# Reload order in the last image, and the place of p's nested weights in image 0: attention and a non-local block on one core

## The chip, the cores and the metric

The kernel runs on one core of one Trainium2 chip. The metric is the device time of one execution in microseconds (us), median of three runs; everything is float32. Five engines work side by side: TensorE (PE: matrix products, with its weight loads as PEld), VectorE (DVE), ScalarE (ACT), GpSimd (POOL) and SyncE (SP), which here starts nearly all transfers. Each engine takes its instructions in the order in which the built program has them.

## The reference

Eight images of 512 channels and 32 x 32 = 1024 positions pass two layers. Cut to what matters:

```python
# layer 0: attention, 8 heads of 64
q, k, v = (conv1x1(x, W, b).reshape(B, 8, 64, N) for W, b in ((Wq, bq), (Wk, bk), (Wv, bv)))
attn = softmax(einsum('bhdn,bhdm->bhnm', q, k) * 64 ** -0.5)
x = x + conv1x1(einsum('bhnm,bhdm->bhdn', attn, v).reshape(B, C, H, W), Wp, bp)
# layer 1: a non-local block, 256 inner channels, then batch normalization over all images
g, theta, phi = (conv1x1(x, W, b) for W, b in ((g_w, g_b), (theta_w, theta_b), (phi_w, phi_b)))
f = einsum('bcn,bdn->bcd', theta, phi) / N
z = conv1x1(einsum('bcd,bdn->bcn', f, g), W_w, W_b) + x
out = (z - mean(z)) * rsqrt(var(z) + 1e-5) * gamma + beta     # over images and positions
```

The mean and the variance of z need all eight images. So z of each image has to be kept until the last image is done, and only then can outputs be written.

## The kernel before, in words

**Stages.** One loop runs over the images. In each turn come attention (`attention`), then q, v and k of the next image (`heads_of`, `values`), the projection p with its residual (`project`), theta and phi together (`theta_phi`, tile `tp`), and the non-local block (`nonlocal_`: g, then f, then z). Products of 512 channels are computed with seven block products in place of eight (`seven`), in the order

```python
SEVEN = (("11", 0, "11", 0, (("11", True),)), ("s1t1", 3, "t1", 1, (("22", True),)),
         ("s2t2", 4, "t2", 0, (("12", True),)), ("s4", 6, "22", 1, (("12", False),)), ...
```

The second entry is the block of the weight, the third the block of the data, the fourth the PSUM slot. The first product uses weight block 0, the second block 3, the third block 4, the fourth block 6. The third adds to the slot of the first, so it waits until VectorE has read that slot. The argument `between` is a dictionary: after the product of that number, and after its PSUM was read, its function puts further instructions into the program.

**Weights.** Blocks 3 to 6 are sums and differences of the four quarters (`weight_sums`, L107). Some products are cut once more, by the same scheme, into blocks of 128 columns; their weights are "nested" (`nest`, L211: four operations of 128 x 128 for each block). In image 0 both kinds are computed, and the finished ones are written to DRAM (`keep`, L206, tensors `kept_...`); from then on they are only loaded (`fetch` L168, called by `load_w`). A weight comes in up to three units: for theta/phi these are blocks 1 and 2 (with nested weights), blocks 3, 4 and 5, and block 6. A unit goes into one of four buffers of pool `wr` and can be loaded only when the unit that was there before has been read for the last time. `load_w` takes the next unit of a list written ahead.

**Queue.** SP starts the transfers in program order. A start that has to wait, for a buffer or for an earlier transfer, holds up all starts behind it. Eight semaphores count landings of these transfers in turn, so each start also waits until the one eight places ahead has landed.

**z.** z of images 0 to 5 is written to DRAM (`spill`), with g and the product W f of images 5 and 6 (`spill_g`). In the last turn they are read back as buffers become free:

```python
def reload(b, pool, tag):            # four transfers of 512 KB (L961)
    t = pool.tile([P, CC, N], F32, tag=tag, name=f"z_{b}")
    for cc in range(CC):
        sp(nc.sync.dma_start(t[:, cc, :], spill[b][:, cc, :]))
```

Images 0, 1, 2 and 3 go to the places of v, q, k and `fold`; image 5 comes in four chunks (`reload_chunks`, L968), then g and W f of images 5 and 6 (`take_back`, L955), image 4 at the end. `last_z` (`late_unit`, L978) computes z of images 5 to 7 chunk by chunk, and `finish` (L1019, L1017, L1020) normalizes all eight and writes them.

**Lines.** Product matmuls stand at L365 (the helper `seven`), nested ones at L313. VectorE's reads of theta/phi's products are L795 (first) and L800 (added), those of p L760 and L471.

## Time and profile before

| | us |
|---|---|
| three runs | 2117.17, 2117.42, 2118.31 |
| median | 2117.42 |
| profiled execution: its time | 2116.34 |
| profiled execution: its span | 2114.6 |
| TensorE busy | 2085.1 |
| VectorE busy | 1428.3 |
| ScalarE busy | 789.9 |
| GpSimd busy | 584.9 |

The span is the time from the first to the last instruction of the profiled execution; its own time holds 1.7 us more around it. Rows of the profile give source line, engine, operation and tiles as out<-in, the count, busy time, mean duration of one, and the idle time before with what ended it. A releaser is the instruction or transfer that ended a wait. The granted clock of TensorE is given as a share of full speed; over the span it is 0.994. A float32 matmul of the source appears as two in the trace.

### The profile page before, as it was taken

The page shows a single profiled execution, that of the slowest core. Times are in us where ns is not written, and L with a number is a line of the kernel's source. Part 1 is how long each engine was busy: PE and PEld are TensorE (multiplying, and loading weights), DVE is VectorE, ACT ScalarE, POOL GpSimd, SP SyncE. Part 2 cuts the span into 40 slices and gives each one's busy share as a digit, 9 for nine tenths or more (in the row PEclk, how much of TensorE's full clock was granted, in tenths as well). Part 3 has the DMA queues.
Part 4 walks back from the last instruction along what each step waited for, and adds up shares of the span by engine and source line. Part 5 has one row for each costly group of instructions (what it writes and reads, how often), then busy time and mean ns, then how long its engine had stood idle before and what let it go on. Part 6 is the DMA issues. An engine that isn't in the chain of part 4 may idle for free.

```text
span 2114.6 us, 33849 instructions
## 1 busy us (share of the span) xinstructions
PE 2085.1 (99%) x13654; PEld 1173.4 (55%) x13654; DVE 1428.3 (68%) x2144; ACT 789.9 (37%) x1045; POOL 584.9 (28%) x454
## 2 busy tenths in 40 slices
PE   9999999999999999999999999999999999999996
PEld 4535864357733677337763377633875348733462
DVE  6587567775678656786567766777665775567736
ACT  1464204642046410564106631166303652066016
POOL 0012900128101371015611156011650129211000
PEclk9999999999999999999999999999999999999998
DMA  6253534244232532425324253232534235222848
GB/s 229 83 148 80 175 115 145 41 93 143 105 116 40 116 115 104 120 41 140 117 73 125 41 153 109 98 95 39 170 129 157 41 73 167 74 32 40 281 181 320
DMA packets 72883, 246.74 MB, mean 117 GB/s; under 512 B 12816, under 2 KB 21264, under 8 KB 70672
## 3 DMA queue, kind: packets, MB, share of 16 engines
q1 hardware_dynamic: 61792, 218.16, 30.6%
q0 software_dynamic: 9072, 24.78, 9.5%
q8 instruction: 110, 1.80, 0.3%
q10 hardware_dynamic: 1856, 1.56, 0.3%
q14 instruction: 53, 0.43, 0.1%
HBM read 163.20 MB, written 47.71 MB: 100 GB/s over the span
## 4 chain that ended last, share of the span: by engine, by line
PE 95%; DMA 2%; DVE 1%; ACT 1%; issue 0%; SPq 0%; DVEq 0%
PE po L627 21%; PE ps L601 21%; PE ptp L365 7%; PE pv_in L441 6%; PE pq_in L444 6%; PE pk_in L444 6%; PE pp L365 6%; PE pg L365 4%; PE pz L365 3%; PE ptp_in_s L313 2%; PE pf L844 2%; PE pp_in_s L316 2%; PE pq L411 1%; PE pv L365 1%; PE pv L408 1%; PE pq L365 1%
## 5 line engine op out<-in xcount | busy, mean ns | idle before, releaser
L604 ACT ACTIVATE e<-ps 128x1024 f32<-128x1024 f32 x512 | 522.6, 1024 | 422.5 <-PE ps L601 411.8
L610 DVE TENSOR_TENSOR acc<-acc,e 128x1024 f32<-128x1024 f32 x384 | 470.0, 1224 | 103.5 <-ACT e L604 94.0
L601 PE MATMUL ps<-q,k 64*64 64x512 f32 x4096 | 529.3, 589 | 0.0
L627 PE MATMUL po<-e,v 64*64 64x512 f32 x4096 | 528.6, 589 | 0.0
L640 POOL DMA_DIRECT2D fold<-acc x189 | 144.7, 766 | 1183.4 <-DMA fold<-acc 753.2
L627 PEld LDWEIGHTS po<-e,v 64*64 64x64 f32 x4096 | 156.6, 133 | 282.9 <-issue 275.7
L601 PEld LDWEIGHTS ps<-q,k 64*64 64x64 f32 x4096 | 155.5, 133 | 283.5 <-issue 275.6
L887 ACT ACTIVATE g<-pg,gb 128x512 f32<-128x512 f32 x31 | 21.3, 687 | 445.8 <-PE pg L365 445.7
L608 DVE TENSOR_TENSOR acc<-e,e 128x1024 f32<-128x1024 f32 x64 | 78.3, 1224 | 118.4 <-ACT e L604 116.2
L365 PE MATMUL ptp<-w_tp,t_x 128*128 128x256 f32 x400 | 98.2, 386 | 6.3 <-DMA w_tp<-kept_tp 6.3
L365 PE MATMUL pp<-t_o,w_WpT 128*128 128x512 f32 x208 | 101.0, 592 | 0.0
L365 PEld LDWEIGHTS ptp<-w_tp,t_x 128*128 128x128 f32 x400 | 73.7, 194 | 15.0 <-issue 6.7
L452 DVE TENSOR_TENSOR v<-v,pv_in 128x256 f32<-128x256 f32 x112 | 46.2, 421 | 43.8 <-PE pv_in L441 37.3
L452 DVE TENSOR_TENSOR k<-k,pk_in 128x256 f32<-128x256 f32 x112 | 46.8, 421 | 39.4 <-PE pk_in L444 34.9
L365 PE MATMUL ptp<-w_tp,x 128*128 128x256 f32 x272 | 69.6, 380 | 0.0
L365 PE MATMUL pp<-o,w_WpT 128*128 128x512 f32 x144 | 67.7, 592 | 0.0
L450 ACT COPY v<-pv_in 128x256 f32<-128x256 f32 x84 | 31.4, 374 | 95.8 <-DVE T_pv L452 25.5
L450 ACT COPY k<-pk_in 128x256 f32<-128x256 f32 x84 | 31.3, 372 | 91.6 <-PE pk_in L444 90.0
L707 POOL TENSOR_TENSOR o<-o,r 128x1024 f32<-128x1024 f32 x28 | 65.2, 2367 | 0.0
L760 DVE SCALAR_TENSOR_TENSOR x<-pp,bp,x 128x512 f32<-128x512 f32 x52 | 37.6, 746 | 33.3 <-PE pp L365 33.3
L441 PE MATMUL pv_in<-w_WvT,i_t_x 128*128 128x128 f32 x448 | 59.2, 275 | 0.0
L444 PE MATMUL pk_in<-i_t_x,w_WkT 128*128 128x256 f32 x224 | 57.8, 381 | 0.0
(246 smaller groups left out, 3118.9 us busy)
## 6 DMA issues: line engine op xcount, KB each, us to landing
fold<-acc POOLq DMA_DIRECT2D x189, 128.0 KB, 3.0
w_WqT<-kept_WqT SPq DMA_DIRECT2D x21, 896.0 KB, 5.7
w_WvT<-kept_WvT SPq DMA_DIRECT2D x21, 896.0 KB, 4.9
w_WkT<-kept_WkT SPq DMA_DIRECT2D x21, 896.0 KB, 5.9
r<-den_d SPq DMA_DIRECT2D x32, 512.0 KB, 6.7
x<-in_x_dram SPq DMA_DIRECT2D x30, 512.0 KB, 6.1
spill<-x SPq DMA_DIRECT2D x24, 512.0 KB, 4.1
z<-spill SPq DMA_DIRECT2D x24, 512.0 KB, 10.4
```

Of the source, the lines that this page charges most:

```text
L365: pe(nc.tensor.matmul(to_ps, lhsT(k), rhs(k), start=(s, at) not in begun, stop=(k == nk - 1), skip_group_check=True))
L441: pe(nc.tensor.matmul(ps[:, i, :], d[:, i * P:(i + 1) * P], a, start=start and not i, stop=True, skip_group_check=True))
L444: pe(nc.tensor.matmul(ps, a, d, start=start, stop=True, skip_group_check=True))
L450: nc.scalar.copy(piece(q, i, j), ps)
L452: dve(nc.vector.tensor_tensor(piece(q, i, j), piece(q, i, j), ps, ALU.add))
L601: pe(nc.tensor.matmul(ps[c * P // 2:(c + 1) * P // 2, j, :], k[r, p, keys], q[r, p, h * 512:(h + 1) * 512], start=True, stop=True, skip_gr ...
L604: nc.scalar.activation(e, ps, AF.Exp, scale=SCALE)
L608: nc.vector.tensor_tensor(accs[u], es[u, 0], e, ALU.add)
L610: ins = nc.vector.tensor_tensor(accs[u], accs[u], e, ALU.add)
L627: pe(nc.tensor.matmul(ps[j * D:(j + 1) * D, r, :], v[keys, m, (2 * p + j) * D:(2 * p + j + 1) * D], e[keys, j, :], start=(m == 0), stop=(m ...
L640: nc.gpsimd.dma_start(to, part_of, accum_op=ALU.add)
L707: dve((engine or nc.vector).tensor_tensor(at, at, of, ALU.mult))
```

## The change

It has two parts, one at each end of the loop.

In the last turn, the reloads of z of images 2 and 3 (eight starts on SP) move from ahead of the projection to behind the loads of the remaining units: theta/phi's second and third unit and g's one unit.

In image 0, the nested weights of p (both blocks) are made after theta/phi's second product, instead of after the third and the fourth; and block 6 of theta/phi's weights is made after the third product instead of after the second. In the built program VectorE then has: read of the second product, eight nest operations, read of the third product, block 6, read of the fourth. Before, it had: read of the second, block 6, read of the third, four nest operations, read of the fourth, four nest operations. On SP the write of p's nested unit comes ahead of that of theta/phi's block 6. No instruction is added or removed.

```diff
             put_away(b - 1)
-            for i, tag in enumerate("vqk"):
+            for i, tag in enumerate("vq"):
                 reload(i, mats, tag)
-            reload(3, foldp, "fold")
         if not last:
             tpb = load_tpb(b)
         w = weights("WpT", sums_done=True)
...
         load_w("first")
         load_w(times=3 if b else 2)
+        if last:
+            reload(2, mats, "k")
+            reload(3, foldp, "fold")
...
         if b == 0:
             weight_sums(w, corner["tp"], (3, 4, 5), dve)

-            between.update({1: lambda: weight_sums(w, corner["tp"], (6,), dve), 2: lambda: nest(w_p, 1),
-                            3: lambda: nest(w_p, 2)})
+            between.update({1: lambda: (nest(w_p, 1), nest(w_p, 2)), 2: lambda: weight_sums(w, corner["tp"], (6,), dve)})
         tp = theta_phi(b, w, data, tpb, between)
```

## The prediction

> **What bounds the kernel now.** I read the page's busy shares first, then the waits of TensorE, then the stages that the change touches as timelines, then the same stage of three images as windows. In the page's part 1 and in the waits (releaser, total us, times, longest):

> ```profile
> PE 2085.1 (99%) x13654; PEld 1173.4 (55%) x13654; DVE 1428.3 (68%) x2144; ACT 789.9 (37%) x1045; POOL 584.9 (28%) x454
> ```

> ```profile
> PE count L1204 <- DVE good L1202: 8.6, 1, 8.6
> PE ptp L365 <- DMA w_tp<-kept_tp: 6.3, 1, 6.3
> ...
> PE pg L365 <- DVE w_WgT L107: 0.7, 1, 0.7
> ```

> TensorE runs back to back for the whole span. A stall put into it or taken out of it moves the end by its own length, as long as the last outputs follow it. The 8.6 us wait is the final check, after the last product. The only large stall is 6.3 us of theta/phi in the last image, on weights still in transfer. Its place on TensorE and on SP's queue (start, length, op, count):

> ```profile
> 2001.34 3.62 PE L365 MATMUL ptp<-w_tp,x 128*128 128x256 f32 x16
> 2011.23 9.20 PE L365 MATMUL ptp<-w_tp,t_x 128*128 128x256 f32 x32 [6.28 <-DMA w_tp<-kept_tp]
> ```

> ```profile
> 1985.41 13.91 SPq L961 DMA_DIRECT2D z<-spill  x12
> 2000.32 1.60 SPq L168 DMA_DIRECT2D w_tp<-kept_tp  x2
> 2002.88 0.32 SPq L168 DMA_DIRECT2D w_WgT<-kept_WgT  x1
> ```

> SP starts sixteen z transfers of 512 KB before it comes to the weights. The chain of waits says why they take so long: each start waits until the transfer eight places ahead has landed.

> ```profile
> 1981.26 7.91 DMA z<-spill
> ...
> 1989.19 11.07 DMA z<-spill
> ...
> 2000.32 10.78 DMA w_tp<-kept_tp
> ```

> The theta/phi stage from its first product to g's first, as windows (length, busy TensorE, granted clock, DMA share, GB/s): images 5 and 6, then 7; and the stall's surroundings.

> ```profile
> 1569.54:1593.12 23.58, 23.58 (x138) 1.00 0.47 176
> 1815.16:1838.75 23.59, 23.59 (x137) 1.00 0.24 80
> 2001.34:2033.48 32.14, 25.86 (x137) 0.89 0.64 249
> ```

> ```profile
> 2008.57:2011.23 2.66, 0.00 (x0) 0.03 (x1) 0.00 (x0) 0.00 (x0) 2.58 (x5) 0.50 1.03 414
> 2011.23:2015.40 4.17, 4.17 (x10) 3.37 (x11) 0.00 (x0) 0.00 (x0) 1.11 (x2) 0.50 1.02 409
> ```

> The stage takes 8.55 us more in image 7. The wait is 6.28; another 4.17 x 0.5 = 2.09 went because the clock had fallen to half and came back only at 2015.40. The rest, 0.2, is the slow first matmuls.

> [...]

> **Part A, the last image.** Eight of the sixteen z starts (images 2 and 3) now follow three weight starts: theta/phi's second unit (768 KB), its third (256 KB) and g's (896 KB). In the built program the second unit's start waits for the first z's landing (1981.26 + 7.91 = 1989.17) and for p's fifth product, whose buffer it takes. p's seven products start at 1977.30 and take 3.43 us each, so that one ends at 1994.5. The third unit waits for the sixth product (1997.9), g's weights for the seventh (2001.34).

> When does the second unit land? Before, the ninth z landed at 2000.26 with eight ahead of it; at 1.28 us for 512 KB (409 GB/s) the eight were in by 1999.0. 768 KB more is 1.9 us: about 2001, the third unit 0.6 later. The second is needed when the first product ends, 2001.34 + 3.45 = 2004.8; the third at 2011.7. The latest I can make it is the longest landing of a z transfer in this stage, 11.7 us: 1994.5 + 11.7 = 2006.2, a stall of 1.4 and too short for the clock. I take no stall.

> What is late next? The third product adds to a bank that VectorE reads from 2006.31 to 2007.53; TensorE reaches it at 2008.24, 0.7 later. GpSimd's inner sums start at 2006.62 and the first four end at 2009.5, before 2011.7. So the stage should take image 6's 23.59: **-8.55 us** for A.

> Behind the wait of g's weights stand eight z, four chunks of image 5's z, WwT and the reloaded g and W f of images 5 and 6. From 2001.34 they are 2.2 us for g's weights and 13 x 1.28 = 16.6: drained near 2020, landed by 2022. The first reloaded g waits for the fourth theta/phi product (start at 2027.04 before, 2018.5 now), the second for a later one. With 12 us to land they are in by about 2036. TensorE reads them at 2052.41 - 8.55 = 2043.9, so the cover is 8 us. z of images 2 and 3 is read first by ScalarE near 2066.1 - 8.55. Without that cover each microsecond late would be a microsecond. The output stage is bound by transfers (399 GB/s from 2070), but between 2040 and 2050 nothing moves and its first output waits for the last image's statistics, so it comes forward too.

> **Part B, image 0.** Nothing is added: four operations of 128 columns for each of two nested blocks, and one sum of 512 columns (w_tp, block 6), change places on VectorE. The order before (timeline of VectorE):

> ```profile
> 286.42 1.23 DVE L795 TENSOR_TENSOR tp<-ptp,tpb 128x1024 f32<-128x1024 f32 x1
> 287.56 0.68 DVE L107 TENSOR_TENSOR w_tp<-w_tp,w_tp 128x512 f32<-128x512 f32 x1
> 289.87 1.23 DVE L795 TENSOR_TENSOR tp<-ptp,tpb 128x1024 f32<-128x1024 f32 x1 [1.63 <-PE ptp L365]
> 291.01 1.26 DVE L211 TENSOR_TENSOR w_WpT<-w_WpT 128x128 f32<-128x128 f32 x4
> ```

> The sum was ready at 288.24; theta/phi's fourth product, which reads it, began at 289.67. In the built order of the changed kernel the read of the second product is followed by all eight nest operations, then the read of the third product, then the sum; the fourth product waits for the sum. So: nests from 287.56, 2 x 1.26 less an overlap of 0.08, to 290.0; the read of the third product (its matmuls are done at 289.87) occupies 1.14 until the next start, 291.15; the sum 0.68, to 291.85; TensorE starts 0.15 later, as after the w_WgT sum (ends 305.91, matmul at 306.06): 292.0. TensorE stalls 292.0 - 289.67 = 2.3 us, and with a slow first matmul **+2.35 us**.

> No later slack takes it up. VectorE's next reads are released by TensorE (idle 1.05, 1.05, 2.2 before them), so they move with it, and the 0.7 us wait for w_WgT hangs on a VectorE chain that starts with such a read. SP writes the nested block back at about 290 instead of 295.75, and the loads behind it start about 4 us earlier; worth nothing, since the only wait of the g stage is on VectorE. Bounds for B: zero is excluded by the order; above, the clock. Gaps of 0.7 us leave it at 1.00 and one of 6.28 halves it; 2.35 is between and unmeasured. One window at half clock would cost 1.7, two 3.4. [...] I take no clock loss.

> **Sum.** -8.55 + 2.35 = -6.2 us. The profiled execution: span 2114.6 to 2108.4, its time 2116.34 to 2110.1. The median of the runs shown is 1.1 above that execution, so 2117.42 - 6.2 = **2111.2 us**.

> **Rivals.**
> 1. The clock halves in image 0 as well. [...] 2111.2 + 1.7 to 3.4 = 2112.9 to 2114.6.
> 2. A new wait takes A's place: the weights land after 2004.8, or the output stage does not come forward. For: weights took 10.8 us to land before, and outputs move at 399 GB/s. Against: half the queue ahead of them is gone, and the stage's start is released by TensorE. If A gives 2 to 6 us, 2113.8 to 2117.8.
> 3. Slower: the reloads behind g's weights come too late for image 5's z at 2043.9. Place: the first pz of image 5. It decides from the moment the second reloaded g lands 8 us after my 2036; it eats the gain at 14 us and is slower than the measurement can miss at 18. For: thirteen transfers are behind one wait now. Against: they need 19 us and have 42. With 20 us late, 2117.42 + 5.8 = 2123.
> 4. The change does not do its part in image 0: the sum is not late. Excluded nearly by the built order; 2117.42 - 8.55 = 2108.9.

> **How the numbers follow.** Likeliest case 0.78, with 2110.2 to 2112.4 of its own (0.5 on each part, 0.5 on the median); rival 1 0.08, rival 2 0.07, rival 3 0.04, rival 4 0.03. 0.2% is 4.2 us, about what a measurement of this kernel can tell from no change: the border is 2113.2. Faster: 0.78 + 0.03 + half of rival 1 + 0.01 of rival 2 = 0.86; same 0.10; slower 0.04. The range takes in the likeliest case and most of rival 1: 2110.0 to 2114.0.

> **What would show it.** Right: no wait of ptp on w_tp in the last image, its stage 23.6 us and clock 1.00 throughout; in image 0 a wait of ptp on DVE w_tp (L107) of about 2.3 us; g's 0.7 us wait unchanged; no wait of pz on gwf or z. Wrong: a half clock after 289 us, any DMA wait after 2001, or a tail from the first output to the end that is longer than before.

## The result, and the profile after

| | before | after |
|---|---|---|
| median, us | 2117.30 | 2110.43 |
| lowest and highest | 2116.31, 2118.31 | 2109.92, 2112.75 |
| executions | 8 | 8 |
| profiled execution: its time | 2116.34 | 2112.45 |
| profiled execution: its span | 2114.6 | 2110.7 |

The ratio of after to before is 0.997, with a 95% interval of 0.9959 to 0.9981: 6.9 us less by the medians. The eight times of after are not spread evenly. Five lie between 2109.92 and 2110.69 and three between 2112.40 and 2112.75, with nothing in between. The profiled execution is one of the upper three, which matters for reading it.

The page's busy shares, and the waits of TensorE (releaser, total us, times, longest), of the changed kernel:

```profile
PE 2085.6 (99%) x13654; PEld 1173.6 (56%) x13654; DVE 1427.4 (68%) x2144; ACT 790.0 (37%) x1045; POOL 585.0 (28%) x454
```

```profile
PE count L1205 <- DVE good L1203: 8.6, 1, 8.6
PE ptp L365 <- DVE w_tp L107: 2.0, 1, 2.0
...
PE pg L365 <- DVE w_WgT L107: 0.7, 1, 0.7
```

The wait on a transfer (6.3 us) is gone, and a wait of 2.0 us on VectorE's sum of w_tp (L107) has come. TensorE's busy time is 0.5 us longer with the same instructions.

**The last image.** TensorE's and SP's timelines of the changed kernel (start, length, op, count):

```profile
2006.06 3.62 PE L365 MATMUL ptp<-w_tp,x 128*128 128x256 f32 x16
2009.51 7.07 PE L365 MATMUL ptp<-w_tp,t_x 128*128 128x256 f32 x32
```

```profile
1985.82 7.46 SPq L961 DMA_DIRECT2D z<-spill  x8
1999.39 3.75 SPq L168 DMA_DIRECT2D w_tp<-kept_tp  x2
2006.25 0.32 SPq L168 DMA_DIRECT2D w_WgT<-kept_WgT  x1
2006.62 6.30 SPq L961 DMA_DIRECT2D z<-spill  x8
```

The second product now starts at 2009.51, when the first ends. Its weights left SP at 1999.39 with eight z transfers ahead of them instead of sixteen; they landed at 2005.30, 4.2 us before they were needed.

**Image 0.** TensorE's and VectorE's timelines of the changed kernel:

```profile
280.17 3.62 PE L365 MATMUL ptp<-w_tp,x 128*128 128x256 f32 x16
283.62 7.07 PE L365 MATMUL ptp<-w_tp,t_x 128*128 128x256 f32 x32
292.65 5.41 PE L365 MATMUL ptp<-w_tp,x 128*128 128x256 f32 x16 [1.96 <-DVE w_tp L107]
```

```profile
287.28 1.23 DVE L795 TENSOR_TENSOR tp<-ptp,tpb 128x1024 f32<-128x1024 f32 x1
288.42 2.44 DVE L211 TENSOR_TENSOR w_WpT<-w_WpT 128x128 f32<-128x128 f32 x8
290.78 1.22 DVE L795 TENSOR_TENSOR tp<-ptp,tpb 128x1024 f32<-128x1024 f32 x1
291.91 0.68 DVE L107 TENSOR_TENSOR w_tp<-w_tp,w_tp 128x512 f32<-128x512 f32 x1
```

VectorE's rows stand in the built order: read at 287.28, eight nest operations at 288.42, read at 290.78, sum at 291.91. In the kernel before, the fourth product begins 10.36 us after the first (279.31 and 289.67); here that would be 290.53. It starts at 292.65, after the sum that ends at 292.59: a gap of 2.12 us. And it takes 5.41 us instead of 3.62, 1.79 more. Of this, 0.10 comes with the gap itself: where the clock stays whole after such a gap, as in the kernel with the sum late below, the product takes 3.72. The half clock is the other 1.69. Windows of the changed kernel (length, busy TensorE, weight loads, VectorE, ScalarE, GpSimd, granted clock, DMA share, GB/s) show why; the first is the last image's theta/phi stage, the others stand around the gap:

```profile
2006.06:2029.63 23.57, 23.57 (x137) 21.38 (x136) 15.39 (x23) 0.00 (x0) 5.61 (x8) 1.00 0.94 355
...
289.99:293.40 3.41, 1.46 (x8) 0.95 (x6) 2.53 (x5) 0.00 (x0) 0.00 (x0) 1.00 0.53 217
293.40:296.81 3.41, 3.41 (x10) 2.65 (x9) 0.00 (x0) 0.00 (x0) 0.00 (x0) 0.50 0.84 267
```

In the last image the stage takes 23.57 us, without a gap and at full clock; it was 32.14. In image 0 the clock fell to half for the 3.41 us after the gap. The stages of the two profiled executions, by their starts:

| | before | after | later by |
|---|---|---|---|
| image 0, first theta/phi matmul | 279.31 | 280.17 | 0.86 |
| image 0, first matmul of g | 303.48 | 308.25 | 4.77 |
| image 7, first theta/phi matmul | 2001.34 | 2006.06 | 4.72 |
| image 7, first matmul of g | 2033.48 | 2029.63 | -3.85 |
| end of the span | 2114.6 | 2110.7 | -3.9 |

Image 0's stage lost 3.91 (2.12 of gap and 1.79 of slower product), image 7's gained 8.57, and between them nothing moved by more than 0.05. The first 0.86 arose ahead of all edits; the last section comes back to it. So this pair of profiles differs by only 3.9 us, and the medians by 6.9.

### The profile page after: what moved, and what is told of

It is laid out like the page before. It is cut to its first block, busy times and chain, and to the rows that moved or that the text cites. A ratio compares the mean times of both kernels' runs of the same rounds, so it can differ in the third digit from the quotient of the medians.

```text
span 2110.7 us, 33849 instructions
## 1 busy us (share of the span) xinstructions
PE 2085.6 (99%) x13654; PEld 1173.6 (56%) x13654; DVE 1427.4 (68%) x2144; ACT 790.0 (37%) x1045; POOL 585.0 (28%) x454
## 3 DMA queue, kind: packets, MB, share of 16 engines
q10 hardware_dynamic: 1856, 1.56, 0.3%
## 4 chain that ended last, share of the span: by engine, by line
PE 97%; DVE 2%; ACT 1%; issue 0%; DMA 0%; DVEq 0%
PE po L627 21%; PE ps L601 21%; PE pp L365 7%; PE ptp L365 6%; PE pv_in L441 6%; PE pq_in L444 6%; PE pk_in L444 6%; PE pg L365 5%; PE pz L365 3%; PE ptp_in_s L313 2%; PE pf L844 2%; PE pp_in_s L316 2%; PE pwf L899 1%; PE pq L411 1%; PE pq L365 1%; PE pv L408 1%
## 5 line engine op out<-in xcount | busy, mean ns | idle before, releaser
L365 PE MATMUL pp<-t_o,w_WpT 128*128 128x512 f32 x208 | 101.0, 592 | 0.0
L365 PE MATMUL ptp<-w_tp,t_x 128*128 128x256 f32 x400 | 96.1, 379 | 0.0
L365 PEld LDWEIGHTS ptp<-w_tp,t_x 128*128 128x128 f32 x400 | 72.3, 191 | 7.8
L365 PE MATMUL ptp<-w_tp,x 128*128 128x256 f32 x272 | 71.4, 387 | 2.0 <-DVE w_tp L107 2.0
L365 PE MATMUL pp<-o,w_WpT 128*128 128x512 f32 x144 | 67.7, 592 | 0.0
```

What stands on the lines that cost most here:

```text
L365: pe(nc.tensor.matmul(to_ps, lhsT(k), rhs(k), start=(s, at) not in begun, stop=(k == nk - 1), skip_group_check=True))
```

## The experiments

Two questions were put first. Does each part do what it was priced at (-8.55 and +2.35), or does one of them hide a loss that the other pays for? And why does the clock halve in some executions: is a gap of some length enough, or does something else decide? All edits are shown against the changed kernel; the ratios are against the kernel before.

### The reload move alone

```diff
-            between.update({1: lambda: (nest(w_p, 1), nest(w_p, 2)), 2: lambda: weight_sums(w, corner["tp"], (6,), dve)})
+            between.update({1: lambda: weight_sums(w, corner["tp"], (6,), dve), 2: lambda: nest(w_p, 1),
+                            3: lambda: nest(w_p, 2)})
```

> The reload move alone; image 0 as before. Theory 1 (the parts add: the move is worth 8.55 us, the part in image 0 costs a gap of TensorE of 2.1 us, and in some executions 1.7 us more of half clock): 2117.3 - 8.5 = 2108.8 us, all executions within about 1 us of each other, no half clock between 280 and 310 us, and 1.5 to 2.5 us faster than the whole change. Theory 2 (the part in image 0 costs nothing in the end, the two groups of times of the changed kernel, about 2110.0 and 2112.5, are noise of the start or the memory): 2110.4 us, the same two groups.

Measured: 2108.17 us (2107.57 to 2108.69, five executions), against 2116.93 of before; ratio 0.9959 (0.9945 to 0.9972). By the medians -8.76. There is one group of times, no wait of theta/phi, and once full, from 4.89 us on, the clock stays whole until TensorE's last products are done. The waits of TensorE in this kernel:

```profile
PE count L1206 <- DVE good L1204: 8.6, 1, 8.6
PE warm_ps L494 <- DVE folds L509: 1.1, 1, 1.1
PE pg L365 <- DVE w_WgT L107: 0.7, 1, 0.7
```

So the gain is all from the reloads, and the order in image 0 only gives some of it back.

### The order in image 0 alone

```diff
-            for i, tag in enumerate("vq"):
+            for i, tag in enumerate("vqk"):
                 reload(i, mats, tag)
+            reload(3, foldp, "fold")
...
-        if last:
-            reload(2, mats, "k")
-            reload(3, foldp, "fold")
```

> The new order in image 0 alone; the last image as before. Theory 1: slower than before by 2.1 us where the clock holds and by 3.9 where one window of half clock follows the gap: 2119.4 to 2121.2. Theory 2: 2117.3. Profile by theory 1: theta/phi waits about 2.0 us for the w_tp sum in image 0 and 6.3 us for w_tp in the last image.

Measured: 2121.36 us (2118.31 to 2122.33, eleven executions); ratio 1.0018 (1.0009 to 1.0027). Slower, and again in two groups: four executions at 2118.31 to 2119.07, seven at 2121.24 to 2122.33. The profiled one (2118.88) is of the lower group; the waits of TensorE in it:

```profile
PE ptp L365 <- DMA w_tp<-kept_tp: 6.1, 1, 6.1
PE ptp L365 <- DVE w_tp L107: 2.0, 1, 2.0
```

The gap is there, 2.0 us, and in image 0 the clock stays at 1.00. So the gap comes from this part. That the upper group has the same gap and a half clock besides is not shown for this kernel; for the changed kernel, the repeated profiles below show it.

### The sum late, without the nested blocks ahead of it

The prediction had the eight nested operations and the sum's new place in one chain. Here the sum stays behind the third product, and the nested blocks go behind it:

```diff
-            between.update({1: lambda: (nest(w_p, 1), nest(w_p, 2)), 2: lambda: weight_sums(w, corner["tp"], (6,), dve)})
+            between.update({2: lambda: (weight_sums(w, corner["tp"], (6,), dve), nest(w_p, 1)),
+                            3: lambda: nest(w_p, 2)})
```

> The reload move, with block 6 of theta/phi's weights made after the third product, and the nested weights of p left where they were (after the third and fourth). It tells which of the two moves in image 0 makes the gap. If it is the sum's place behind the read of the third product: read released at the third product's end, 1.14 us, then 0.68 us of sum, a wait of 1.8 us and about 2110.2 to 2112. If it is the eight nest operations ahead of that read: no gap, 2108.8 us.

Measured: 2112.25 us (2109.81 to 2112.91, eleven executions: five up to 2110.29, six from 2112.25 on); ratio 0.9974 (0.9965 to 0.9983). TensorE's and VectorE's timelines of this kernel:

```profile
291.95 3.72 PE L365 MATMUL ptp<-w_tp,x 128*128 128x256 f32 x16 [1.92 <-DVE w_tp L107]
```

```profile
290.07 1.23 DVE L795 TENSOR_TENSOR tp<-ptp,tpb 128x1024 f32<-128x1024 f32 x1 [2.23 <-PE ptp L365]
291.21 0.68 DVE L107 TENSOR_TENSOR w_tp<-w_tp,w_tp 128x512 f32<-128x512 f32 x1
```

VectorE was idle for 2.23 us before the read of the third product, so nothing was late, and the recorded wait is still 1.92, against 1.96 in the changed kernel. The gap is the time that VectorE takes to read a finished product (1.14) and to make the sum (0.68) with the step to TensorE, because the sum stands behind a read of the product just before the one that needs it. The nested blocks ahead of it can add no more than the rest, 0.04 us.

### The nested blocks early, the sum ahead of them

```diff
-            between.update({1: lambda: (nest(w_p, 1), nest(w_p, 2)), 2: lambda: weight_sums(w, corner["tp"], (6,), dve)})
+            between.update({1: lambda: (weight_sums(w, corner["tp"], (6,), dve), nest(w_p, 1), nest(w_p, 2))})
```

> The reload move, with block 6 back after the second product and the nested weights made right behind it, ahead of the read of the third product. If the sum's place makes the gap: no wait, 2108.8 us as with the reload move alone, and the write of p's nested unit still starts about 4 us earlier than before, for no gain. If the nest operations make it: a wait of 2 us and 2110.5 us or more.

Measured: 2108.25 us (2107.53 to 2108.76, five executions); ratio 0.9958 (0.9945 to 0.9972). No wait of theta/phi, and one group of times. The early nested blocks cost nothing, and bring nothing over the reload move alone (2108.17).

### A shorter gap

The sum is cut in two: its first 256 columns are made after the second product, the rest after the third. The second nested block goes back behind the fourth product.

```diff
-            between.update({1: lambda: (nest(w_p, 1), nest(w_p, 2)), 2: lambda: weight_sums(w, corner["tp"], (6,), dve)})
+            def half_of_6(k):
+                dve(nc.vector.tensor_tensor(w[6][:, k, :], w[1][:, k, :], w[4][:, k, :], ALU.subtract))
+
+            between.update({1: lambda: (half_of_6(0), nest(w_p, 1)), 2: lambda: half_of_6(1), 3: lambda: nest(w_p, 2)})
```

> The reload move, with block 6 of theta/phi's weights made in two halves: the first after the second product, the second after the third. TensorE can do two matmuls of the fourth product and then waits some 1.4 us. Theory 1 (the clock halves when about 2 us or more of one 3.41 us window are idle): never a half clock, all executions in one group, 2108.2 + 1.6 = 2109.8 us. Rival (any gap behind the third product can halve the clock, or the two groups come from elsewhere): two groups about 2.4 us apart, as with the gap of 2.1 us.

Measured: 2109.65 us (2109.33 to 2110.29, six executions); ratio 0.9966 (0.9953 to 0.9978). The wait fell to 1.22, for two reasons: the second half is shorter, and two matmuls of the fourth product, which read the first half, ran ahead of the gap. TensorE's timeline of this kernel:

```profile
289.70 0.59 PE L365 MATMUL ptp<-w_tp,x 128*128 128x256 f32 x2
291.51 3.29 PE L365 MATMUL ptp<-w_tp,x 128*128 128x256 f32 x14 [1.22 <-DVE w_tp L1164]
```

The median is 7.5 us below that of before in the same set (2117.16), where the reload move alone was 8.76 below its own: the difference, about 1.25, is the gap itself. There is no upper group.

### A longer gap

Block 4 is made twice more, with the same values, ahead of the sum.

```diff
-            between.update({1: lambda: (nest(w_p, 1), nest(w_p, 2)), 2: lambda: weight_sums(w, corner["tp"], (6,), dve)})
+            between.update({1: lambda: (nest(w_p, 1), nest(w_p, 2)),
+                            2: lambda: [weight_sums(w, corner["tp"], (i,), dve) for i in (4, 4, 6)]})
```

> The whole change, with block 4 of theta/phi's weights computed twice more (the same values) ahead of block 6, so that the gap is some 1.3 us longer, 3.3 us. Theory 1: 2111.6 us where the clock holds and 2113.3 to 2114.2 where it halves for a window, and it halves in most executions, about four in five, against 16 of 30 with the gap of 2.1 us. Rival (the two groups have nothing to do with the gap): the same share of about half, or one group at 2113.

Measured: 2112.95 us (2111.28 to 2115.61, seventeen executions); ratio 0.9981 (0.9973 to 0.9988). Five executions lie at 2111.28 to 2111.57, about 1.5 above the changed kernel's lower group, which fits the longer gap alone; eight at 2111.92 to 2113.57; four at 2114.34 to 2115.61. The profiled one (2113.57) waits 3.41 us, at full clock until 294.97. Windows of this kernel:

```profile
291.55:294.97 3.42, 1.34 (x6) 1.21 (x7) 1.96 (x3) 0.00 (x0) 0.00 (x0) 1.00 0.94 385
294.97:298.38 3.41, 3.41 (x10) 2.71 (x9) 0.00 (x0) 0.00 (x0) 0.00 (x0) 0.50 0.96 292
```

By these times the clock halves in twelve of seventeen executions, against 16 of 30 in the kernels with the gap near 2 us so far; that is no clear difference, and five seem to escape. Only one execution was profiled. The mean granted clocks on record point the same way (0.996 in all five, 0.994 in the two highest), but two of the middle eight have 0.996 too: they are too coarse to count windows. What the four highest lost is not shown.

### One reload moved, and all four

With the order of before in image 0, only image 3's reload is moved:

```diff
-            for i, tag in enumerate("vq"):
+            for i, tag in enumerate("vqk"):
                 reload(i, mats, tag)
...
         if last:
-            reload(2, mats, "k")
             reload(3, foldp, "fold")
```

> Image 0 as before; of the two reloads only that of image 3 is moved, image 2's four transfers stay ahead of theta/phi's weights. Theory (what counts is the bytes ahead of the weights): 4 x 1.28 us later than with both moved, so theta/phi's second unit lands about 1 us after it is needed; a wait of 0.9 to 1.3 us in the last image, no half clock, 2108.2 + 1.1 = 2109.3 us. If it is the starts that wait for the eighth transfer before them that count: no wait, since the weights' start comes no later (it waits for p's fifth product either way), 2108.2.

Measured: 2109.73 us (2109.21 to 2110.89, six executions); ratio 0.9967 (0.9954 to 0.9979). TensorE's timeline of this kernel:

```profile
2006.20 7.14 PE L365 MATMUL ptp<-w_tp,t_x 128*128 128x256 f32 x32 [1.35 <-DMA w_tp<-kept_tp]
```

The weights' start was not held up: SP issued it at 1994.6, when its buffer came free. But it took 11.5 us to land, behind twelve z transfers; in the changed kernel, behind eight, it took 5.9. What counts is the bytes ahead in the queue, more than the place of the start.

With all four moved, and image 0 again as before:

```diff
-            for i, tag in enumerate("vq"):
-                reload(i, mats, tag)
...
         if last:
-            reload(2, mats, "k")
+            for i, tag in enumerate("vqk"):
+                reload(i, mats, tag)
             reload(3, foldp, "fold")
```

> Image 0 as before; all four reloads (images 0 to 3) are moved behind the weights. Tells how much cover the reloads behind g's weights have. Theory: eight transfers more are 10.2 us more behind the wait for p's last product; the last reloaded g and W f that the first z of image 5 needs come 5 us or more before TensorE reads them: no wait, 2108.2 us. If the cover is smaller than 10 us, as the prediction's estimate of 8 us had it: a wait of pz on gwf of up to 2 us, up to 2110.5.

Measured: 2108.01 us (2107.56 to 2108.56, four executions); ratio 0.9958 (0.9942 to 0.9973), the same as with two. The unit landed 4.0 us after its start. At the other end, the second reloaded g landed at 2039.67 and was read at 2044.30: 4.6 us of cover are left, and no wait appears. In the changed kernel it landed at 2034.63 and was read at 2048.55, a cover of 13.9. Of the numbers tried, one is too few, and two and four are safe at both ends; three was not run.

### The changed kernel four times more, for the phase

The profiles so far suggested that the clock is decided in windows of 3.413 us that follow one another without a break: in each profile, every later change of the clock falls a whole number of windows after full clock first comes. The length is read from the trace's records of the granted clock: in the first profile of the changed kernel full clock comes at 6.68, half at 293.40, full at 296.81 and half at 2092.22, which is 84, 85 and 611 times 3.4133 us after the first; in the kernel before, it comes at 4.95, and the half clock from 2008.57 to 2015.40 is the windows 588 and 589 after that. The same kernel, unedited, was profiled four times:

> The changed kernel again, for the phase of the clock's windows. Theory (the windows of 3.413 us run on from the launch; a window halves the clock when about 2 us of it, or more, are idle): with e the time at which full clock first comes, windows end at e + n x 3.4133. The gap stands at about 289.7 to 291.8 where e is near 5 and at 290.5 to 292.6 where e is near 7, so it lies in one window, and the clock halves in image 0 for 3.41 us, where e lies between about 5.1 and 7.2 (time near 2112.4); with e between 4.0 and 4.9 the gap is cut by an edge, and the clock holds (near 2110.0). Rival (the length of the gap decides, which varies by chance): a half clock appears with no relation to e, and the gap is longer where it does.

> As the run before it. About half of the executions halve the clock: by e between 5.1 and 7.2 by the theory, by the length of the gap by the rival.

> As the run before it. About half of the executions halve the clock: by e between 5.1 and 7.2 by the theory, by the length of the gap by the rival.

> As the run before it. About half of the executions halve the clock: by e between 5.1 and 7.2 by the theory, by the length of the gap by the rival.

Measured: 2112.29, 2112.49, 2110.67 and 2110.06 us. The clock halved in image 0 in the first two, and never before the end of TensorE's work in the others: all four as expected from the time of the first full clock (5.98, 6.70, 4.33 and 4.86). Two windows each of the second and the fourth:

```profile
290.00:293.42 3.42, 1.47 (x8) 0.96 (x7) 2.53 (x5) 0.00 (x0) 0.00 (x0) 1.00 0.53 216
293.42:296.83 3.41, 3.41 (x10) 2.65 (x9) 0.00 (x0) 0.00 (x0) 0.00 (x0) 0.50 0.89 283
```

```profile
288.16:291.58 3.42, 1.63 (x8) 1.10 (x6) 3.28 (x8) 0.00 (x0) 0.00 (x0) 1.00 0.24 101
291.58:294.99 3.41, 3.25 (x15) 2.89 (x16) 0.11 (x1) 0.00 (x0) 0.00 (x0) 1.00 0.95 322
```

All profiles with such a gap, with the time of the first full clock (from the trace's records of the clock), the wait, and TensorE's busy time in the window of this grid that holds most of the gap:

| kernel | first full clock | wait | busy in the window | clock after it |
|---|---|---|---|---|
| a longer gap | 4.84 | 3.41 | 1.34 | half |
| changed, first of the four | 5.98 | 1.96 | 1.45 | half |
| changed, first profile | 6.68 | 1.96 | 1.46 | half |
| changed, second of the four | 6.70 | 1.95 | 1.47 | half |
| changed, fourth | 4.86 | 1.95 | 1.63 | whole |
| sum late | 5.06 | 1.92 | 1.66 | whole |
| changed, third | 4.33 | 1.96 | 2.10 | whole |
| image 0 alone | 4.40 | 1.95 | 2.19 | whole |
| a shorter gap | 5.01 | 1.22 | 2.20 | whole |

The rival, that a longer gap by chance halves the clock, falls: the same kernel with waits of 1.95 and 1.96 gave both outcomes. The busy time in one window puts all nine in order, with the border between 1.47 and 1.63 of 3.41 us. The windows at the end of TensorE's work, on the same grids, agree and narrow it: 1.56, 1.61 and 1.66 us of work (first and third of the four, reload move alone) left the next window whole, 1.16, 1.20 and 1.23 (all four moved, changed kernel, second of the four) halved it. Where an edge cuts the gap, as in the third run, neither window is idle enough: 2.77 and 2.10 us of work were left in the two, and the clock stayed at 1.00. The phase differs from execution to execution, and that makes the two groups of times of the changed kernel.

The five escapes with the longer gap fit this too. In the profiled execution that gap began 10.52 us after theta/phi's first matmul. Put there, as an estimate, into the starts and grids of all fourteen profiles, a gap of 3.41 us is cut so near its middle in five of them that both windows keep 1.57 us of work or more, and in a sixth they keep 1.55. Five or six of fourteen is no less than five of seventeen.

## Why the prediction was right, and where not

**The forecast.** 2111.2 was given, 2110.43 measured, and the sign and the mechanism of the gain are as argued. But 2111.2 stands between the two groups, at a time that none of the eight executions took, and the median is 2110.43 because five of them fell into the lower group; the middle of the upper one is 2112.45. So the closeness is in part luck: the half clock was left out, and the lower group gained about 1 us more than the terms give (see the sum below).

**Part A: right.** -8.55 was predicted for the stage and -8.57 measured; the part alone gave -8.76 by the medians. The step under it, when the second unit lands, held too: "about 2001" with the first product at 2001.34, so 0.3 ahead of it. It landed 0.76 ahead (2005.30 against 2006.06). The 1.4 us stall kept as a bound came true where one reload fewer moved, 1.35 us with a landing time of 11.5, and there it left the clock alone: the product behind it took 7.14 us, against 7.07 in the changed kernel without a wait.

**"What is late next": right in direction, mis-sized.** No wait of pz on a reload came, and the output stage came forward: from g's first matmul of the last image to the end it is 81.1 us in both. The second reloaded g, set at 2036, landed on the same scale at 2029.9 (2034.63 less the 4.72 by which the stage now starts later), so the cover was 13.9 and not 8. The estimate gave each transfer 12 us to land; the first three reloaded g and W f took 5.7 to 8.2 (with all four moved, 11.6 to 12.2).

**Part B, the gap: right.** 2.35 was predicted with a slow first matmul; the gap measured 2.12, with the slower product after it 2.22. Term by term: nested operations 2.44 (2.44 predicted), the read 1.13 (1.14), the sum 0.68, and from the sum to TensorE 0.06 where 0.15 had been taken from another place. What the prediction's own numbers said but its text did not draw out: the nested operations cost only 0.13 of this (290.0 against 289.87). The sum's place behind the third read makes nearly all of it, as the kernel with the sum late shows.

**Part B, "I take no clock loss": wrong, in 5 of the 12 executions of the changed kernel** (three by their profiles, two by their times alone). A half clock after 289 us was one of the prediction's own signs of being wrong. The failed step is that a gap which the prediction itself calls unmeasured was given no loss; that was the author's estimate, and the profile of before didn't show it: it has gaps of 0.7 us at full clock and one of 6.28 with half clock, and none near 2. The runs fill this in: 1.95 us was enough where it fell into one window, since a window with 1.45 to 1.47 us of TensorE's work in it halved the next one. The size "one window at half clock would cost 1.7" was right: 1.69 (5.41 less 3.72). Rival 1 had been given 0.08, an estimate too; the executions with such a gap split about evenly (5 of 12 here; 7 of 11 with image 0 alone and 6 of 11 with the sum late, if their upper groups are this).

**The sum.** -6.2 was predicted. With whole clock the parts measured give -8.57 + 2.12 + 0.10 = -6.35, with half clock -4.66. Between executions of nearly the same phase this comes out: the fourth repeat, in another set of runs, with its first full clock at 4.86, took 2110.06, 6.28 less than the profiled execution of before, with 4.95 (2116.34). Against the median of before the lower group's middle, 2109.99, is -7.3 and the upper group's, 2112.45, is -4.85. The rest of the lower group, about 1 us, is what the median of before (2117.30) stands above its profiled execution; why executions of before differ (2116.31 to 2118.31) isn't shown.

**Rivals 2, 3 and 4** did not come about. Rival 3's mechanism was tested with all four reloads moved, and still had 4.6 us to spare.

## What to carry to other kernels

On an engine that runs back to back, a sum that feeds the next product must not stand behind the read of the product just before it: that order costs the read and the sum together (1.92 to 1.96 us of wait here), however early the engine was free. Where weights are late, count the bytes queued ahead of them (the same 768 KB took 4.0 to 11.5 us to land here), and move only as much behind them as the next reader's cover allows. A gap on TensorE should be priced with its clock: near 2 us (1.92 to 1.96 here) it was a matter of phase, so time several executions and look for groups before trusting one profile; here the reload move alone, or with the sum kept ahead of the nested blocks, is about 2 us better than the whole change.
